# A gated recurrent kernel on one core: the biases and h0 on ScalarE's DMA queue, the banks zeroed from a tile of zeros

## The chip, the cores and the metric

The kernel runs on one core of a Trainium2 chip. The metric is the device time of one execution in microseconds (us), the median of several runs. A core has a matrix engine (TensorE, in the profile PE, with its weight loads as PEld), VectorE (DVE), ScalarE (ACT), GpSimd (POOL) and SyncE (SP). SP computes nothing here: it issues DMA transfers. [...]

## What is computed

The input x holds 8 sequences of 512 steps with 512 features; h0 is the first state, 8 by 512. Cut to what matters:

```
def step(h, x_t):
    fused = sigmoid(concat([x_t, h]) @ w_W + w_b)
    r, z  = split(fused, 2)
    m     = x_t @ wx_W + wx_b + r * (h @ wh_W + wh_b)
    h_new = z * h + (1 - z) * tanh(m)
    return h_new
out = x + all h_new, step after step
```

All of it is float32. The steps depend on each other. Only the products with x can be made ahead.

## The kernel before

The kernel's loop has 512 steps, one for each step of the sequences, all of the same work. The weights are kept in SBUF for the whole run: `wx` (for x) and `wh` (for h), each loaded by four DMAs of 768 KB, one for each quarter k of the 512 features. The units of the state lie in four quarters too: half A (`hTA`) and half B (`hTB`) hold two each. x comes in chunks of 16 steps (`xin`, 256 KB each, `load_x`, line 76), loaded three chunks ahead; the results go out in tiles `ot` of the same size.

A group is four steps. For each group, `seed` (line 155) copies the biases into a PSUM bank `xp`, `prefill` (line 159) adds x times `wx` to it, and `spread` (line 171) copies the parts to the banks A, B and Z, on which the products with h are summed. The banks alternate between groups. `turn_x` (line 176) transposes the part for the candidate state.

A step begins with 48 matmuls of h with `wh`, in the order of line 23, "A0 B0 A1 A2 A3 B1 B2 B3 Z0 Z1 Z2 Z3": the letter is the bank, the figure the quarter k of `wh` and of h. One quarter of the prefill for the group after next follows (`take(pre, 1)`, line 217). Then VectorE transposes the sums, ScalarE makes the sigmoids and the tanh, VectorE forms the new state by two scans (`memory`, line 261, `update`, line 281), half A before half B, and GpSimd adds x for the output. The next step's A0 waits for the new `hTA`, its A2 for the new `hTB`.

The loop's order is fixed by hand (line 199). The part ahead of it, the prologue, is ordered by a scheduler, in the order of the code where nothing else decides. There SP issues, by lines 83 to 96, 123 and 189: four transfers of biases (each a row of 512 values to 32 partitions), the first chunk of x, four of `wx`, four of `wh`, h0 (tile `hin`), and the next chunks of x. The DMAs have eight semaphores which they take in turn, so an issue can also wait for the transfer that had its semaphore before.

On the other engines the prologue does this. GpSimd sets `zeros`, the state tiles and some helper tiles to zero, VectorE the first `DVE_FILL` = 5 of the helper tiles (lines 111 to 115). VectorE copies `hin` into the first state (line 125). TensorE clears each of the eight PSUM banks with four matmuls, of a tile of zeros with the biases (line 143); this also marks the banks as begun, since all later matmuls only add. Then follow the seeds, the prefills of the first two groups and the spread of the first. ScalarE loads a table of functions ahead of its first copy (line 157) and another ahead of its first sigmoid (line 150).

Of the kernel before, what the change touches and what calls it, by code (L numbers as in the profile page):

```python
# [7 lines left out]
F32 = mybir.dt.float32  # L8
# [4 lines left out]
P = 128  # L13
NQ = 4
GS = 4
B = 8
HU = 64


DVE_FILL = 5  # L20
SYNC = mybir.DependencyInfo(mybir.DependencyClass.Sync, mybir.DependencyReason.DATA)

ORDER = "A0 B0 A1 A2 A3 B1 B2 B3 Z0 Z1 Z2 Z3"
# [7 lines left out]
def tile_cond_rnn_residual(  # L31
# [31 lines left out]
    nc = tc.nc  # L63
# [4 lines left out]
    const = ctx.enter_context(tc.tile_pool(name="const", bufs=1))  # L68
# [7 lines left out]
    def load_x(c):  # L76
        if c < NCH:
            t_ = xin_p.tile([P, NQ, TC * B], F32, tag="xin", name=f"xin_{c}")
            nc.sync.dma_start(out=t_, in_=x[c].rearrange("p (k n) -> p k n", k=NQ))  # L79
            xins[c] = t_  # L80


    bias = const.tile([P, 512], F32, name="bias")
    for j in range(NQ):
        nc.sync.dma_start(  # L85
            out=bias[32 * j : 32 * j + 32], in_=bias_d[j].partition_broadcast(32)
        )
    load_x(0)

    wx = const.tile([P, NQ, NQ, 384], F32, name="wx")  # L90
# [3 lines left out]
    wh = const.tile([P, NQ, NQ, 384], F32, name="wh")  # L94
    for k in range(NQ):
        nc.sync.dma_start(out=wh[:, k], in_=wh_d[:, k])

    NH = 2 * GS  # L100
    hT = [
        [const.tile([P, 32, 2, 2], F32, name=f"hT{n}{i}") for i in range(NH)]
        for n in "AB"
    ]
# [3 lines left out]
    hd0 = [[const.tile([P, B, 2, 2], F32, name=f"hd0{n}{i}") for i in range(2)] for n in "AB"]  # L108
    hd1 = [[const.tile([P, B, 2, 2], F32, name=f"hd1{n}{i}") for i in range(2)] for n in "AB"]
    zs = [[const.tile([P, 2, B], F32, name=f"z{n}{i}") for i in range(2)] for n in "AB"]  # L110
    zeros = const.tile([P, 32], F32, name="zeros")
    for t_ in [zeros] + hT[0] + hT[1]:
        nc.gpsimd.memset(t_, 0.0)
    for n, t_ in enumerate(hd0[0] + hd0[1] + md0[0] + md0[1]):
        (nc.vector if n < DVE_FILL else nc.gpsimd).memset(t_, 0.0)

# [2 lines left out]
        s = i % GS  # L119
        return hT[hf][i % NH][:, B * s : B * s + B, :, 1]  # L120

    hin = const.tile([P, NQ, B], F32, name="hin")
    nc.sync.dma_start(out=hin, in_=h0)
    for hf in range(2):
        nc.vector.tensor_copy(  # L125
            state(hf, 0), hin[:, 2 * hf : 2 * hf + 2].rearrange("p c b -> p b c")
# [8 lines left out]
    def mm(out_, lhsT, rhs, start=False):  # L135
        nc.tensor.matmul(  # L136
            out_, lhsT, rhs, start=start, stop=False, skip_group_check=True
        )


    for t_ in xps + list(banks[0].values()) + list(banks[1].values()):
        for j in range(NQ):
            mm(t_[32 * j : 32 * j + 32, :], zeros, bias[:, : t_.shape[1]], start=True)

# [39 lines left out]
                return  # L186
            n = None if n is None else n - 1

    load_x(1)
    load_x(2)  # L190
    for g in range(2):
        seed(g)
        take(prefill(g))
# [191 lines left out]
```

## Time and profile before

| | us |
|---|---|
| median of 3 runs | 1726.7 |
| lowest and highest run | 1726.22, 1728.58 |
| profiled execution | 1726.31 |
| its span, first to last instruction | 1724.5 |
| TensorE busy | 1706.2 |
| VectorE, ScalarE, GpSimd busy | 1138.6, 894.8, 252.9 |
| first matmul of the loop | 22.80 |

Times in the profile are counted from the start of the span. In a timeline, a row has start, length, engine, line, operation, output and inputs, count, and in brackets how long the engine was idle before it and what ended that. "SPq" is SP's queue issuing DMAs. The chain of waits follows the execution back from its last instruction, at each step to what released it. The granted clock (PEclk) is 1.00 at full speed of TensorE. All matmuls of the kernel have line 136, that of a helper, so they are told apart by tile: A, B, Z for the banks, xp for the prefill.

### The profile page before, as it was taken

Reading aid. Unit: us, or ns where it says so; the run is one execution under the profiler, and the core shown is the slowest. Engines: PE = TensorE matmul, PEld = TensorE weight load, DVE = VectorE, ACT = ScalarE, POOL = GpSimd, SP = SyncE. Lnnn points to the kernel's source line nnn. Section 1 sums busy time; section 2 is a strip of 40 time slices with the busy share of each in tenths; the row PEclk is TensorE's granted clock in tenths of the full one; section 3 lists DMA queues with packets and bytes.
Section 4 is the critical chain, followed back from the end, with each engine's and each line's share of the span. In section 5 each row is a group of like instructions: output and inputs, shape, how many; then the busy total and the mean of one; then the engine's idle time right before and its main releaser. Section 6 shows DMA issues by size and latency. Waiting matters only on the chain.

```text
span 1724.5 us, 121032 instructions
## 1 busy us (share of the span) xinstructions
PE 1706.2 (99%) x53312; PEld 1489.8 (86%) x53312; DVE 1138.6 (66%) x6663; ACT 894.8 (52%) x4610; POOL 252.9 (15%) x1048
## 2 busy tenths in 40 slices
PE   7999999999999999999999999999999999999998
PEld 5888888888888888888888888888888888888887
DVE  2666666666666666666666666666666666666666
ACT  3555555555555555555555555555555555555554
POOL 1111111111111111111111111111111111111111
PEclk9999999999999999999999999999999999999999
DMA  4000000000000000000000000000000000000000
GB/s 179 17 4 17 17 17 17 10 11 17 17 17 16 5 17 17 17 16 5 17 17 17 17 17 5 17 17 17 17 4 17 16 17 16 5 17 11 11 11 10
DMA packets 11232, 31.09 MB, mean 18 GB/s; under 512 B 1360, under 2 KB 1360, under 8 KB 10704
## 3 DMA queue, kind: packets, MB, share of 16 engines
q1 hardware_dynamic: 10704, 23.35, 3.9%
q8 instruction: 416, 6.82, 1.6%
q14 instruction: 112, 0.92, 0.2%
HBM read 14.96 MB, written 8.39 MB: 14 GB/s over the span
## 4 chain that ended last, share of the span: by engine, by line
PE 98%; DMA 1%; DVE 0%; issue 0%; SPq 0%; ACT 0%; POOLq 0%; POOL 0%; DVEq 0%
PE A L136 39%; PE B L136 25%; PE xp L136 19%; PE Z L136 14%; DMA hin<-in_h_dram 1%; DMA wx<-in_wx_dram 0%; DVE tr L231 0%; ACT md0A L150 0%; DVE hTA L283 0%; DVE m L263 0%; SPq L85 0%; DVE md L243 0%; SPq L79 0%; POOLq L379 0%; POOL ot L314 0%
## 5 line engine op out<-in xcount | busy, mean ns | idle before, releaser
L136 PE MATMUL A<-wh,hTA 128*32 128x192 f32 x8192 | 555.6, 327 | 9.5 <-DVE hTB L125 7.3
L136 PEld LDWEIGHTS A<-wh,hTA 128*32 128x32 f32 x8192 | 321.3, 137 | 184.6 <-DVE hTA L283 176.2
L136 PE MATMUL B<-wh,hTA 128*32 128x128 f32 x8192 | 450.9, 273 | 0.0
L136 PE MATMUL A<-wh,hTB 128*32 128x192 f32 x8192 | 448.3, 327 | 0.0
L136 PE MATMUL xp<-wx,xin 128*32 128x384 f32 x4096 | 444.2, 486 | 0.0
L231 DVE STREAM_TRANSPOSE tr<-A 128x64 f32<-128x64 f32 x512 | 128.0, 250 | 470.0 <-PE A L136 470.0
L150 ACT ACTIVATE md0A<-tr 128x16 f32<-128x16 f32 x512 | 121.1, 236 | 487.9 <-DVE tr L231 487.9
L136 PEld LDWEIGHTS B<-wh,hTA 128*32 128x32 f32 x8192 | 364.7, 136 | 1.6
L136 PE MATMUL B<-wh,hTB 128*32 128x128 f32 x8192 | 336.4, 273 | 0.0
L136 PEld LDWEIGHTS A<-wh,hTB 128*32 128x32 f32 x8192 | 302.4, 137 | 33.0 <-DVE hTB L283 1.2
L314 POOL TENSOR_TENSOR ot<-xin,hTA 128x16 f32<-128x16 f32 x512 | 125.5, 245 | 1119.5 <-DVE hTA L283 1031.6
L136 PEld LDWEIGHTS B<-wh,hTB 128*32 128x32 f32 x8192 | 266.6, 137 | 0.0
L136 PE MATMUL Z<-wh,hTB 128*32 128x64 f32 x8192 | 240.6, 226 | 0.0
L136 PE MATMUL Z<-wh,hTA 128*32 128x64 f32 x8192 | 235.0, 223 | 0.0
L136 PEld LDWEIGHTS Z<-wh,hTA 128*32 128x32 f32 x8192 | 218.5, 141 | 0.0
L136 PEld LDWEIGHTS Z<-wh,hTB 128*32 128x32 f32 x8192 | 200.1, 148 | 0.0
L314 POOL TENSOR_TENSOR ot<-xin,hTB 128x16 f32<-128x16 f32 x512 | 124.5, 243 | 348.5 <-DVE hTB L283 343.2
L150 ACT ACTIVATE md0B<-tr 128x16 f32<-128x16 f32 x512 | 119.2, 233 | 70.8 <-DVE tr L231 0.7
L283 DVE TENSOR_TENSOR_SCAN hTB<-hd0B,hd1B 128x32 f32<-128x32 f32 x512 | 115.2, 225 | 52.7
L263 DVE TENSOR_TENSOR_SCAN m<-md0B,md 128x32 f32<-128x32 f32 x512 | 147.6, 288 | 0.0
L243 DVE STREAM_TRANSPOSE md<-B 128x64 f32<-128x64 f32 x512 | 146.9, 287 | 0.0
L243 DVE STREAM_TRANSPOSE md<-A 128x64 f32<-128x64 f32 x512 | 139.0, 271 | 0.0
(43 smaller groups left out, 1835.8 us busy)
## 6 DMA issues: line engine op xcount, KB each, us to landing
xin<-in_x_dram SPq DMA_DIRECT2D x32, 256.0 KB, 2.9
out_dram<-ot SPq DMA_DIRECT2D x32, 256.0 KB, 2.1
wx<-in_wx_dram SPq DMA_DIRECT2D x4, 768.0 KB, 6.7
wh<-in_wh_dram SPq DMA_DIRECT2D x4, 768.0 KB, 13.5
bias<-in_bias_dram SPq DMA_DIRECT2D x4, 64.0 KB, 2.0
hin<-in_h_dram SPq DMA_DIRECT2D x1, 16.0 KB, 14.8
```

The costliest lines, as they stand in the source:

```text
L136: nc.tensor.matmul(out_, lhsT, rhs, start=start, stop=False, skip_group_check=True)
L150: inst = nc.scalar.activation(*args, **kw).ins
L231: nc.vector.transpose(t_.rearrange("p c n -> p (c n)"), raw[n][hf])
L243: inst = nc.vector.transpose(md1[g % 2][:, hf, :, :, 0].rearrange("p n c -> p c n"), raw["h"][hf]).ins
L263: nc.vector.tensor_tensor_scan(flat(m), flat(md0[hf][g % 2][:, rows]), flat(md1[g % 2][:, hf, rows]), 0.0, ALU.mult, ALU.add,)
L283: nc.vector.tensor_tensor_scan(flat(hT[hf][(i + 1) % NH][:, B * s1 : B * s1 + B]), flat(hd0[hf][i % 2]), flat(hd1[hf][i % 2]), 0.0, ALU.mu ...
L314: pool_done[i + 1] = nc.gpsimd.tensor_tensor(ot[:, 2 * hf : 2 * hf + 2, t, :].rearrange("p c n -> p n c"), xins[c][:, 2 * hf : 2 * hf + 2, ...
```

## The change

The four transfers of biases, and the one of h0, are issued by ScalarE's queue instead of SP's, and h0 directly after the biases. The second and third chunk of x are asked for in the code directly after `wh`. The tile `zeros` is 512 wide instead of 32, is filled by VectorE, and stands on both sides of the matmuls that clear the banks, so the biases are no longer read there. `DVE_FILL` goes from 5 to 4: with it the first tile `md0A`, the input of the first candidate scan, is cleared by GpSimd.

```diff
-DVE_FILL = 5
+DVE_FILL = 4
...
     bias = const.tile([P, 512], F32, name="bias")
     for j in range(NQ):
-        nc.sync.dma_start(
+        nc.scalar.dma_start(
             out=bias[32 * j : 32 * j + 32], in_=bias_d[j].partition_broadcast(32)
         )
+    hin = const.tile([P, NQ, B], F32, name="hin")
+    nc.scalar.dma_start(out=hin, in_=h0)
     load_x(0)
...
     for k in range(NQ):
         nc.sync.dma_start(out=wh[:, k], in_=wh_d[:, k])
+    load_x(1)
+    load_x(2)
...
-    zeros = const.tile([P, 32], F32, name="zeros")
-    for t_ in [zeros] + hT[0] + hT[1]:
+    zeros = const.tile([P, 512], F32, name="zeros")
+    nc.vector.memset(zeros, 0.0)
+    for t_ in hT[0] + hT[1]:
         nc.gpsimd.memset(t_, 0.0)
...
-    hin = const.tile([P, NQ, B], F32, name="hin")
-    nc.sync.dma_start(out=hin, in_=h0)
...
-            mm(t_[32 * j : 32 * j + 32, :], zeros, bias[:, : t_.shape[1]], start=True)
+            mm(t_[32 * j : 32 * j + 32, :], zeros[:, :32], zeros[:, : t_.shape[1]], start=True)
...
-    load_x(1)
-    load_x(2)
     for g in range(2):
         seed(g)
         take(prefill(g))
```

## The prediction

> **What bounds the kernel now.** I read the page first (its busy shares, then its chain of waits), then the timeline of the first 28 us, then the chain and the windows of that stretch.
>
> ```profile
> PE 1706.2 (99%) x53312; PEld 1489.8 (86%) x53312; DVE 1138.6 (66%) x6663; ACT 894.8 (52%) x4610; POOL 252.9 (15%) x1048
> PE 98%; DMA 1%; DVE 0%; issue 0%; SPq 0%; ACT 0%; POOLq 0%; POOL 0%; DVEq 0%
> ```
>
> TensorE makes up 98% of the chain, and that is the loop: 512 steps of about 3.31 us each (the distance of the transposes of A in the timeline). The diff touches nothing inside the loop, so only the prologue can move the end. Its DMA issues and the moments that matter, from the timeline:
>
> ```profile
> 0.74 1.78 SPq L85 DMA_DIRECT2D bias<-in_bias_dram  x4
> 2.56 0.42 SPq L79 DMA_DIRECT2D xin<-in_x_dram  x1
> 4.93 2.06 SPq L96 DMA_DIRECT2D wh<-in_wh_dram  x4
> 7.62 0.33 SPq L123 DMA_DIRECT2D hin<-in_h_dram  x1
> 9.51 4.09 SPq L79 DMA_DIRECT2D xin<-in_x_dram  x3
> 16.80 1.28 ACT L150 ACT_TABLE_LOAD   x1
> 26.07 0.25 DVE L231 STREAM_TRANSPOSE tr<-A 128x64 f32<-128x64 f32 x1 [3.31 <-PE A L136]
> 26.36 0.24 ACT L150 ACTIVATE md0A<-tr 128x16 f32<-128x16 f32 x1 [8.27 <-DVE tr L231]
> 27.30 0.23 DVE L283 TENSOR_TENSOR_SCAN hTA<-hd0A,hd1A 128x32 f32<-128x32 f32 x1
> ```
>
> See three things here. SP spends 1.78 us on issuing biases before the first x. The later chunks of x (9.51) are already issued behind wh (4.93). And the activation table for the sigmoid is loaded at 16.80, long before the first sigmoid needs it at 26.36. The chain of the same stretch:
>
> ```profile
> 7.62 14.81 DMA hin<-in_h_dram
> 22.80 0.88 PE A L136 x8
> 23.67 0.43 PE B L136 x8
> 24.10 1.92 PE A L136 x24
> 26.02 0.77 PE B L136 x24
> 26.79 0.49 PE Z L136 x32
> 27.28 0.64 PE xp L136 x8
> 27.92 0.33 PE A L136 x8
> ```
>
> The 16 KB of h0 land 14.81 us after their issue, at 22.43, since they stand behind all of wh. Step 0 then runs from 22.80 to 27.92. What wh itself does, from the view of that tensor, for its last two issues (6.0 and 6.5 us):
>
> ```profile
> DMA to landing us min/median/max: 14.2/15.0/15.7
> ```
>
> So wh3 lands at 6.5 + 15.7 = 22.2, only 0.2 us ahead of h0. This is the main reading: h0 is named by the chain, but the weights bind. The windows (columns: stretch, length, busy us of PE, PEld, DVE, ACT, POOL, then granted clock, DMA share, GB/s):
>
> ```profile
> 15.89:19.30 3.41, 0.00 (x0) 0.00 (x0) 0.22 (x3) 1.87 (x2) 0.00 (x0) 1.00 1.01 416
> 19.30:22.72 3.42, 0.00 (x0) 0.00 (x0) 0.20 (x2) 0.00 (x0) 0.00 (x0) 0.50 0.87 330
> 22.72:26.13 3.41, 3.33 (x48) 2.61 (x52) 0.10 (x2) 0.00 (x0) 0.00 (x0) 0.50 0.02 7
> 26.13:29.54 3.41, 3.41 (x113) 2.90 (x109) 2.29 (x13) 1.79 (x9) 0.49 (x2) 1.00 0.02 5
> ```
>
> The DMA engines are full until the weights are in. TensorE's clock fell to half during its idle time, and stayed there for the first 3.33 us of step 0.
>
> [...]
>
> **The change part by part.**
>
> 1. Biases leave SP's queue. SP's first issue becomes xin0, at 0.74 instead of 2.56, so the stream of x, wx and wh starts 1.8 us earlier. The four bias transfers don't vanish: 256 KB at the stream's 416 GB/s is 0.6 us. In the kernel before they moved before the stream; now they share the engines with it. That gives back 0 us (if they fill the stream's first latency) to 0.6 us. I take 0.6. wh3 then lands at 22.2 - 1.8 + 0.6 = 21.0. wh0 lands at 15.1 (4.9 + 10.2, the shortest of the four); three transfers more at 768 KB/416 GB/s = 1.9 us would take 5.7 us, and they took 7.1. The other 1.4 us I put down to one instruction fetch of 16 KB that the DMA view shows in 14.5 to 18. [...] I keep it.
>
> 2. h0 leaves SP's queue and the end of the stream. It is issued on ScalarE after the biases at about 2.6, and VectorE's two copies (0.18 and 0.17 us at 22.5) become free. This takes away the named wait, but the next is 1.2 us earlier at best (22.2 to 21.0), because wh3 is late next.
>
> 3. What starts without wh3. The matmuls of step 0 stand in the order A0 B0 A1 A2 A3 ..., one chunk of wh each. With h0 there, A0, B0, A1 and A2 run as wh0, wh1, wh2 land (the stream moved by 1.2: about 14, 17 and 19 us). Before, they cost 0.88 + 0.43 + 1.28 = 2.6 us after 22.80; now only A3 stands after wh3. A3 at half clock is 1.92/3 = 0.64 (24 rows are three quarters k of A), plus 0.24 of start (0.88 less 0.64): A ends at 21.05 + 0.88 = 21.9, against 26.02. Behind it B1 to B3, Z and xp took 0.77 + 0.49 + 0.64 = 1.90 at full clock. At half clock they take 3 x 0.43 + 2 x 0.43 + 2 x 0.64 = 3.4. Step 1 starts at 21.9 + 3.5 = 25.4 instead of 27.92: a gain of 2.5, if the half clock lasts just that long (4.4 us from 21.05).
>
> 4. The clock. A1 and A2 are 0.3 to 0.6 us of work in stretches of 2 us, so I expect half clock when wh3 lands: in 1719.14 to 1722.55 the same view has 0.78 us of TensorE, and the clock still fell after it (mean 0.76 in 1721 to 1724). [...] the half clock lasts 3.4 us from 21.05 at best and 6.8 at worst, mean 5.1. Each us of it costs half a us of work: the gain is 2.5 + 0.5 = 3.0, 2.5 - 1.2 = 1.3, and 2.15 in the mean.
>
> 5. Later chunks of x behind wh. Nothing: the issue order is already so, and in the changed program's order SP has x0, wx, wh, x1, x2. xin1 is first needed by the prefill in step 8, some 27 us into the loop.
>
> 6. Banks zeroed from zeros. TensorE's first matmul waits for one memset of 128x512 on VectorE. The 128x128 one takes 0.17 and the 128x32 one 0.09 to 0.12, so about 0.4 us, up at 1.3, in place of the biases at 4.30. The zeroing (32 matmuls, 4.30 to 9.6) starts 3 us earlier and the prefill follows the landing of wx. It ends near 13.2 (before: 15.49). All of this is hidden under the wait for wh, which is the cover: alone it saves nothing; were wh early, it would save up to 3 us. Memsets of GpSimd: one of 32 columns goes, one of 128 (0.20) comes, over by 3.7 us, hidden by the same.
>
> 7. The table load moves. The fill of the first md0A goes from VectorE to GpSimd (DVE_FILL 4), so the first sigmoid waits for two engines. In the changed program's order ScalarE waits for VectorE's transpose of A first, then loads the table, then waits for GpSimd. Before, the load had no wait ahead of it. So 1.28 us stand between the transpose and the sigmoid in step 0; behind them queue zA, hd0A, tanh, and VectorE's scan. hTA comes 26.02 to 27.53 = 1.51 us after A; now 1.51 + 1.28 = 2.8, at 24.7. At half clock TensorE is busy with B, Z and xp until 25.4, so the load is hidden; at full clock it costs up to 1.3[...]. In the best clock case (window done at 24.45) xp ends at 24.9 and some 0.15 is lost. I take 0, range 0 to 0.9.
>
> ScalarE's five DMA issues (2.1 us by SP's rate of 0.45 each) end at 2.9, before its first wait ends at 4.2. Hidden.
>
> Sum: -2.2 us, against the profiled execution's own 1726.31 (span 1724.5 and 1.8 around it): 1724.1. The median of the runs is 1726.7, 0.4 above it; [...] I sum from it with the mean clock of the changed kernel.
>
> **The rivals.** (A) as above. (B) The stream ends earlier: the biases hide in its first latency, or the late engine isn't late; 0.6, 1.4 or 2.0 us more, of which I take 1.3: 1722.8. (C) The clock stays full through the short bursts: A ends at 21.5, xp at 23.3, but then the table load shows: hTA at 21.5 + 2.8 = 24.3, step 1 at about 24.6, a gain of 3.3: 1723.0. Against it speaks the window with 0.78 us. (D) The gain stays away: bias and x packets slow each other, or the clock rises late (6.8 us)[...]: gain 0.5 to 1, 1725.6. (E) Slower: SP's issue of wx2 now waits on a semaphore that ScalarE's first bias transfer returns, in the changed program. SP's queue holds x0, wx0 and wx1 until then, about 4.4 us of stream, to some 7 us. If ScalarE's transfers start late, the stream starves, one us lost for each us; past a bias landing of 9.2 (7 plus the gain of 2.2) the kernel is slower. At 10.5 it would be 1727.6. Before, the first bias landed 2 us after its issue, which speaks against it.
>
> **How the numbers follow.** A 0.58, B 0.13, C 0.12, D 0.13, E 0.04. A alone spans 1723.1 to 1725.3: gains of 3.0 to 1.3, with 0.2 to 0.3 for wh3's landing. The range runs from 1722.5, taking in most of B and C, to 1725.9, over D. Two tenths of a per cent, about what a measurement of this kernel can tell from no change, is 3.5 us, so faster means under 1723.2: a tenth of A, most of B and two thirds of C, 0.27 with a little for a gain that I don't see. Slower by that much needs more than E: 0.04. The rest, 0.69, is within.
>
> **What would show it.** h0 lands before 7 us and no longer ends the chain; wh3's landing near 21.0 does; A0, B0, A1 and A2 run apart before it. The transpose of A starts near 22 instead of 26.07. A table load of 1.28 us stands between that transpose and the first sigmoid. Step 1 starts between 24.5 and 26.5. Steps stay at 3.31 us. I am wrong if wh3 lands outside 20.4 to 21.6, if the clock at 21 us is full, or if the steps change.

## The result, and the profile after

The changed kernel takes 1723.17 us in the median (1722.18 to 1724.39, 13 runs), the kernel before 1727.14 us in the same measurement (1726.22 to 1728.97, 13 runs). The ratio is 0.9976, with a 95% interval of 0.9967 to 0.9984: 0.24% or 4.0 us faster. In a second measurement (`r_after` below) it is 1722.35 against 1725.76, ratio 0.9981 (0.9973 to 0.9989). The forecast was 1724.1, within 1722.5 to 1725.9.

The profiled executions are 1726.31 before and 1723.64 after, 2.67 us apart. First the chain of waits of the changed kernel, in the prologue (start, length, what):

```profile
2.12 6.55 DMA bias<-in_bias_dram
...
8.68 12.54 DMA wh<-in_wh_dram
...
21.26 0.70 PE A L139 x8
21.97 1.28 PE B L139 x24
23.25 0.85 PE Z L139 x32
24.10 1.14 PE xp L139 x8
25.24 0.33 PE A L139 x8
```

h0 is gone from it. The biases stand in it because SP's last issue, that of wh3 (the last quarter of wh), waits for the semaphore of the last bias transfer; the DMA engines were full meanwhile (share 1.02 in 3.50 to 8.70 us, 1.00 in 8 to 10 us), so this cost nothing. The last quarter of wh ends the wait now, at 21.22, and only one group of A (8 rows, k = 3) stands behind it, where the chain before had all four from 22.80. Step 1 starts at 25.24 instead of 27.92: 2.68 us earlier, the whole difference of the two executions. From there on nothing changed: the mean step from the ninth on is 3.3118 us before and 3.3116 after. Now the timeline of the same stretch:

```profile
1.45 3.40 PE L139 MATMUL xp<-zeros 128*32 128x512 f32 x16 [1.45 <-DVE zeros L116]
8.76 1.28 ACT L160 ACT_TABLE_LOAD   x1 [8.76 <-DMA bias<-in_bias_dram]
10.69 7.06 PE L139 MATMUL xp<-wx,xin 128*32 128x384 f32 x64 [4.53 <-ACT xp L160]
22.02 0.25 DVE L232 STREAM_TRANSPOSE tr<-A 128x64 f32<-128x64 f32 x1 [3.63 <-PE A L139]
22.35 1.28 ACT L153 ACT_TABLE_LOAD   x1 [3.28 <-DVE tr L232]
24.45 0.23 DVE L284 TENSOR_TENSOR_SCAN hTA<-hd0A,hd1A 128x32 f32<-128x32 f32 x1
```

The transpose of A is at 22.02 (before 26.07), the table load stands behind it, and hTA is ready at 24.68, while TensorE is busy until 25.24. One thing was not expected: the biases land at 8.67 and the prefill begins at 10.69, a microsecond later than before (9.67), although the banks are cleared 3 us earlier. In between TensorE had nothing to do for 4.53 us; its clock was at half (0.50) from 11.31 to 14.72, and the 64 matmuls of the prefill took 7.06 us where they had taken 5.82. From the DMA views, KB each and median us to landing, of the kernel before:

```profile
bias<-in_bias_dram SPq DMA_DIRECT2D x4, 64.0 KB, 2.0
```

and of the changed kernel:

```profile
bias<-in_bias_dram ACTq DMA_DIRECT2D x4, 64.0 KB, 5.1
hin<-in_h_dram ACTq DMA_DIRECT2D x1, 16.0 KB, 8.0
```

### The profile page after: what moved, and what is told of

It is laid out like the page before. It is cut to its first block, busy times and chain, and to the rows that moved or that the text cites. A ratio compares the mean times of both kernels' runs of the same rounds, so it can differ in the third digit from the quotient of the medians.

```text
span 1721.9 us, 121031 instructions
## 1 busy us (share of the span) xinstructions
PE 1707.1 (99%) x53312; PEld 1484.6 (86%) x53312; DVE 1138.9 (66%) x6663; ACT 894.6 (52%) x4610; POOL 254.6 (15%) x1048
## 4 chain that ended last, share of the span: by engine, by line
PE 98%; DMA 1%; DVE 0%; issue 0%; ACT 0%; ACTq 0%; POOLq 0%; POOL 0%
PE A L139 39%; PE B L139 25%; PE xp L139 19%; PE Z L139 14%; DMA wh<-in_wh_dram 1%; DMA bias<-in_bias_dram 0%; DVE tr L232 0%; ACT md0A L153 0%; DVE hTA L284 0%; DVE m L264 0%; DVE md L244 0%; ACTq L85 0%; POOLq L380 0%; POOL ot L315 0%; DVE hd1A L275 0%
## 5 line engine op out<-in xcount | busy, mean ns | idle before, releaser
L153 ACT ACTIVATE zB<-tz 128x16 f32<-128x16 f32 x512 | 110.8, 216 | 53.9
```

The source lines that it names most:

```text
L153: inst = nc.scalar.activation(*args, **kw).ins
```

## The experiments

All twelve were timed beside the kernel before; a ratio is to it, in the same measurement. Its median there lay at 1725.8 to 1726.0, 1.2 to 1.4 us under that of the first measurement, so ratios are compared and not times across measurements. "Changed" means the changed kernel.

**`e1_bias_back`: the biases on SP again.**

```diff
-        nc.scalar.dma_start(
+        nc.sync.dma_start(
             out=bias[32 * j : 32 * j + 32], in_=bias_d[j].partition_broadcast(32)
```

> The changed kernel with the four bias transfers back on SP's queue, ahead of x; h0 stays on ScalarE's. My theory: the landing of the last quarter of wh ends the prologue, so this costs what the stream starts later: wh3 at 22.2 instead of 21.2, the transpose of A in step 0 near 23.0 instead of 22.0, 1724.2 us. Rival: the gain is that of h0 alone, which the chain of waits named: then nothing is lost, 1723.2 us.

Measured: 1723.34 us, ratio 0.9985 (0.9979 to 0.9992), 2.6 us under the kernel before and 0.7 to 1.6 us over the changed one by its two ratios (0.9981 and 0.9976). Its chain:

```profile
6.47 15.43 DMA wh<-in_wh_dram
...
21.94 0.88 PE A L139 x8
```

wh3 lands 0.7 later than in the changed kernel (21.22), less than the 1.0 expected, and still ends the prologue. So moving h0, with the biases left on SP, brings most of the gain, since it frees three of the four groups of A; moving the biases brings the rest. The intervals of the ratios overlap, so the second part is shown by the landing rather than by the times.

**`e2_h0_back`: h0 behind wh again.**

```diff
+    hin = const.tile([P, NQ, B], F32, name="hin")
+    nc.sync.dma_start(out=hin, in_=h0)
     for hf in range(2):
...
-    nc.scalar.dma_start(out=hin, in_=h0)
```

(The two later chunks of x stand behind it, as in the kernel before.)

> The changed kernel with h0 back on SP's queue behind wh (and the later chunks of x behind h0); the biases stay on ScalarE's. My theory: h0 lands at about 21.4, the first matmul of the loop starts at 21.7, and A0 to A2 stand on the path again: step 0 about 1.1 us ahead of the kernel before, 1726.0 us. Rival (the gain is the earlier start of the stream alone): 1723.2 us.

Measured: 1726.1 us, ratio 1.000 (0.9992 to 1.0008). The gain is gone; the 1 us that I expected to stay doesn't show, though it would still lie within the interval of 1.4 us to either side. The timeline of the profiled execution and, below the dots, its chain:

```profile
25.26 0.25 DVE L232 STREAM_TRANSPOSE tr<-A 128x64 f32<-128x64 f32 x1 [3.30 <-PE A L137]
25.59 1.28 ACT L151 ACT_TABLE_LOAD   x1 [6.73 <-DVE tr L232]
27.69 0.22 DVE L284 TENSOR_TENSOR_SCAN hTA<-hd0A,hd1A 128x32 f32<-128x32 f32 x1
...
27.34 0.80 PE xp L137 x8
28.14 0.39 PE A L137 x8
```

Step 0 does start 0.8 us earlier than before (at 21.99, before at 22.80), and the transpose of A is 0.8 us earlier. After that, two things delay step 1. The table load, which the change put there, takes 1.28, so that hTA is ready at 27.91, after the 27.53 of the kernel before. And the half clock lasted until 27.52 (before: 26.13), so that TensorE itself was at work until 28.14, where step 1 starts; by the chain it was this that set the start here, 0.2 us later than the load would have. Which of the two takes the gain in the other runs is not shown. So h0's move is necessary, and the earlier stream brings nothing measurable without it.

**`e3_fill5`: md0A cleared by VectorE again.**

```diff
-DVE_FILL = 4
+DVE_FILL = 5
```

> The changed kernel with DVE_FILL 5 again, so that the first md0A is cleared by VectorE and the table load has no wait ahead of it. My theory: in the changed kernel the load lies beside TensorE's half-clock work, so that 0 to 0.4 us is won: 1723.0 us. Rival: its 1.28 us are on the path: 1721.9 us.

Measured: 1722.34 us, ratio 0.9979 (0.9970 to 0.9988), equal to the changed kernel within the intervals; the runs spread over 3 us (1720.36 to 1723.52). This doesn't decide alone. Its profile, one of the fastest of its runs (1721.22), shows the clock at full through the whole of step 0; from its windows (columns as in the prediction):

```profile
17.82:21.23 3.41, 1.69 (x40) 1.02 (x40) 0.54 (x4) 2.07 (x4) 0.00 (x0) 1.00 0.98 391
21.23:24.65 3.42, 3.42 (x108) 2.86 (x112) 2.23 (x13) 1.80 (x9) 0.48 (x2) 1.00 0.07 23
```

and from those of the changed kernel:

```profile
18.13:21.55 3.42, 1.41 (x35) 0.74 (x28) 0.26 (x3) 0.59 (x1) 0.00 (x0) 1.00 0.92 364
21.55:24.96 3.41, 3.41 (x72) 2.59 (x68) 1.53 (x10) 2.29 (x7) 0.15 (x1) 0.50 0.04 13
```

The same work, cut by stretches that fall otherwise: behind the one with 1.69 us of TensorE the clock was 1.00, behind the one with 1.41 it was 0.50 for 3.41 us.

**`e4_zero_back`: the banks cleared with the biases again.**

```diff
-            mm(..., zeros[:, :32], zeros[:, : t_.shape[1]], start=True)
+            mm(..., zeros[:, :32], bias[:, : t_.shape[1]], start=True)
```

> The changed kernel, but the banks are cleared with the biases as the moving operand again, so TensorE waits for the biases, which land at 8.7. My theory: the clearing starts at 8.7 and the prefill ends near 18.5, A0 to A2 fit before wh3 lands at 21.2, and since TensorE has less idle time its clock may be full then: 1722.5 to 1723.2 us. Rival: the earlier clearing is where the gain is from: 4 us later prefill, 1725 us or more.

Measured: 1722.36 us, ratio 0.9981 (0.9973 to 0.9989), equal to the changed kernel. The prefill runs from 13.06 to 18.41 instead of 10.69 to 17.75, and A0 to A2 still end before wh3 lands at 21.18. The earlier clearing of the banks brings nothing measurable. The clock was full from 11.39 on, and then the table load was in the chain (22.18 to 23.47), with step 1 at 24.56.

**`r_after`: the changed kernel again.**

> The changed kernel itself once more, beside the others of this call. Theory of the clock's windows: its profile falls in another place of the windows, so the half clock after wh3's landing lasts between 0 and 5 us; the times spread over some 2 us, and the ratio to the kernel before stays between 0.997 and 0.9985. If the half clock is tied to the kernel and not to free windows, its profile is as the first: half from about 21.5 to 25.0 us.

Measured: ratio 0.9981 (0.9973 to 0.9989). In its profile the clock fell at 22.04, 0.86 us after wh3's landing (0.3 in the first profile), after a stretch of 3.41 us with 1.38 us of TensorE. A3 ran at full clock, the half clock lasted into step 1 (25.46), and step 1 started at 24.82, 0.4 us earlier than in the first profile. So the place of the half clock is not fixed by the kernel: 21.55 to 24.96 in the first profile, 22.04 to 25.46 in this one.

**`e6_hold` and `e7_hold_fill5`: the clock kept up, without and with the table load out of the way.** Both put matmuls of zeros into the waits of step 0, which add zeros to bank xp1; the second also has DVE_FILL 5.

```diff
+HOLD = {"A2": (384,), "A3": (512, 192)}
...
+            for w in HOLD.get(n, ()) if i == 0 else ():
+                for j in range(NQ):
+                    mm(xps[1][32 * j : 32 * j + 32, :w], zeros[:, :32], zeros[:, :w])
```

> The changed kernel with three groups of matmuls of zeros put into TensorE's waits ahead of A2 and A3 of step 0 (they add zeros to a bank). Theory: [...] its clock is full when wh3 lands in every run; A ends at 21.6, but the table load is then on the path and step 1 starts at 24.6 instead of 25.05: 0.4 to 0.8 us faster than the changed kernel in the median, with a smaller spread. Rival: the clock does not matter, because the table load lies beside it anyway: no difference.

> The same matmuls of zeros, and DVE_FILL 5, so neither the half clock nor the table load is in step 0. Theory: step 1 starts at 23.3 in every run, 1.2 us ahead of the hold alone and 1.7 us ahead of the changed kernel. Rival: the load costs nothing, and this is equal to the hold alone.

Measured: 1721.31 us, ratio 0.9973 (0.9963 to 0.9983), and 1720.23 us, ratio 0.9967 (0.9955 to 0.9979). The clock was full in both profiles: 1.00 in 18.62 to 22.03 of the first, with 3.16 us of TensorE, and 24 rows of B took 0.66 in the second, where the changed kernel at half clock has 1.28. The chains differ as expected. With the hold alone, ScalarE's load is in it:

```profile
22.13 1.28 ACT L154
...
24.51 0.56 PE A L140 x8
```

With DVE_FILL 5, TensorE runs through:

```profile
22.95 0.65 PE xp L140 x8
23.60 0.33 PE A L140 x8
```

Between the two lies 1.1 us in the medians and 0.9 in these chains: at full clock the table load costs that, while in the changed kernel, at half clock, hTA was ready at 24.68, ahead of the end of TensorE's work at 25.24. The spread fell from 2.4 us (`r_after`, 14 runs) to 0.6 and 0.4 (8 and 6 runs). The step of the expectation that failed: of the 1.0 us between the hold and `r_after`, 1.4 are in the loop (mean step 3.3080 against 3.3108 us, times 504), not in step 0. Within what these runs tell, full clock with the table load on the path (step 1 at 24.51) was worth as much here as half clock with the load hidden (24.82 in `r_after`).

**`e5_wide_clear`: fewer instructions ahead of the loop.**

```diff
-        for j in range(NQ):
-            mm(t_[32 * j : 32 * j + 32, :], zeros[:, :32], zeros[:, : t_.shape[1]], start=True)
+        mm(t_, zeros[:, :P], zeros[:, : t_.shape[1]], start=True)
```

> The changed kernel, but each bank is cleared by one matmul with 128 columns of zeros as weights instead of four with 32, so 96 of the 128 instructions of the clearing are gone. Theory that the fetch of TensorE's instructions delays one DMA engine by 1.4 us: the fetch now comes only after TensorE is past its wait for wh3, wh3 lands at 19.8 instead of 21.2, and the kernel is about 1.4 us faster, 1.4 to 1.9 if less idle time also keeps the clock up. Rival (the late engine has another cause, such as its place in the memory): wh3 stays at 21.2 and the time the same.

Measured: 1719.84 us (1719.65 to 1720.00), ratio 0.9965 (0.9952 to 0.9977), 2.5 us under `r_after` in the same measurement. The chain:

```profile
8.17 11.73 DMA wh<-in_wh_dram
...
19.94 0.60 PE A L139 x8
```

wh3 lands 1.3 us earlier, and the fetch that the trace had at 14.5 to 14.7 in the changed kernel now comes at 21.1. This supports the fetch as what makes one DMA engine late; the last section has the other profiles on it. The rest of the 2.5 is again in the loop: mean step 3.3080.

**`e10_before_wide`: the same edit in the kernel before.** There it is `mm(t_, zeros, bias[:, : t_.shape[1]], start=True)` with zeros of 128 columns.

> The kernel before with one change: each bank is cleared by one matmul with 128 columns of zeros. Theory of the instruction fetch: it moves behind TensorE's wait for h0, so the weights and h0 land 1.4 us earlier, at 20.8 and 21.0, and step 0 starts at 21.4: 1.4 us faster than the kernel before. Rival (the late engine belongs to the order of the changed kernel or to the place of wh in memory): no difference.

Measured: 1723.23 us, ratio 0.9983 (0.9977 to 0.9990), 2.7 us faster, twice the expected gain. wh3 landed at 20.84 and h0 at 21.02, step 0 started at 21.39: 1.4 us earlier, as expected. In this profile, the slowest of its 21 runs, the half clock lasted until 27.26, so step 1 started only 0.2 us earlier than before; the mean step of 3.3078 instead of 3.3118 gives 2.0 us over the loop. This one edit in the prologue's TensorE work, with nothing of the change, is worth 0.7 to 0.9 of what the change is, by the ratios (0.9983 against 0.9976 and 0.9981).

**`e11_wide_padded`: what is in the loop?** This is `e5_wide_clear`, but the 24 matmuls that it saves come back as matmuls of zeros where TensorE is idle under the table load.

```diff
         take(pre, 1)
+        for _ in range(6) if i == 0 else ():
+            for j in range(NQ):
+                mm(xps[1][32 * j : 32 * j + 32, :HU], zeros[:, :32], zeros[:, :HU])
```

> The wide clearing, with the 24 matmuls that it saves given back as matmuls of zeros behind the prefill of step 0, where TensorE is idle for 1 us under the table load; so the number of TensorE's instructions from step 1 on is that of the changed kernel. Theory: the wide clearing has two gains; the landing of wh3 at 19.9 stays, but the four to seven long steps (3.4 to 4.0 us, each the second step of a chunk of 16) come back[...]: mean step 3.310 to 3.312 us and 1721.2 us, 1.4 above the wide clearing alone. Rival: the long steps belong to the matmuls of the old clearing or to chance: mean step 3.308 us and 1719.8 us.

Measured: 1721.61 us, ratio 0.9976 (0.9967 to 0.9985). wh3 landed at 19.99, so the prologue's gain stayed; the mean step is 3.3098, and long steps are back. Counted are steps over 3.4 us after the eighth, from the distances of the transposes of A:

| kernel | long steps | mean step, us |
|---|---|---|
| before; changed; `r_after` | 6; 6; 5 | 3.3118; 3.3116; 3.3108 |
| `e1`; `e2`; `e3`; `e4` | 4; 3; 4; 4 | 3.3103; 3.3108; 3.3100; 3.3108 |
| `e5`; `e6`; `e7`; `e8`; `e9`; `e10` | 0; 0; 1; 0; 0; 0 | 3.3080; 3.3080; 3.3083; 3.3076; 3.3079; 3.3078 |
| `e11` | 3 | 3.3098 |

Each of them is the second step of a chunk of 16. They go, but for one in `e7`, wherever TensorE's instructions ahead of the loop are other in number, and come back when the number does. Each count is from one execution.

**`e8_wide_fill5` and `e9_wx_pieces`.** The first is the wide clearing with DVE_FILL 5, the second the same with the rows of wx padded.

```diff
-    wx = const.tile([P, NQ, NQ, 384], F32, name="wx")
+    wx = const.tile([P, NQ, NQ, 400], F32, name="wx")
...
-        nc.sync.dma_start(out=wx[:, k], in_=wx_d[:, k])
+        nc.sync.dma_start(out=wx[:, k, :, :384], in_=wx_d[:, k])
```

(The matmuls of the prefill read `wx[:, k, j, :384]` to match.)

> The changed kernel with the wide clearing of the banks and DVE_FILL 5. Theory: the wide clearing brings wh3 to 19.9 with a full clock, where the table load is wholly on the path; with DVE_FILL 5 the load is early and step 1 starts at 22.0 instead of 23.3: 1.2 us under the wide clearing alone, 7 us under the kernel before. Rival: something else is late at once (the scan for half B, say) and at most 0.4 us is won.

> As the wide clearing with DVE_FILL 5, but the rows of wx in SBUF are padded from 384 to 400 values, so that wx comes in pieces of 1536 bytes instead of 6144, in the same four DMAs. Theory: [...] with pieces of a quarter of the size the biases land at about 5 us instead of 8.2 and the prefill starts at 7 to 8; the time is the same within 0.4 us, since wh3 still ends the prologue. Rival (ScalarE's queue is slow by itself[...]): the biases land at 8 again.

Measured: `e8_wide_fill5` 1719.18 us, ratio 0.9962 (0.9950 to 0.9975). It is the fastest of all by its ratio, 6.7 us under the kernel before, but not told apart from the wide clearing alone (0.9965): by the medians 0.7 us of the expected 1.2. In its profile wh3 came at 20.31, 0.4 later than in `e5`, and step 1 started at 22.70 instead of 23.27, so the table load is off the path, as expected. `e9_wx_pieces` 1719.97 us, ratio 0.9964 (0.9952 to 0.9976), with runs from 1717.45 to 1722.48. Its DMA view:

```profile
bias<-in_bias_dram ACTq DMA_DIRECT2D x4, 64.0 KB, 4.8
hin<-in_h_dram ACTq DMA_DIRECT2D x1, 16.0 KB, 6.2
```

The pieces of wx were 1536 bytes, and the last bias landed at 8.3 all the same. So smaller pieces of wx did not bring the biases to the 5 us that I had expected; h0, behind them, came 1.6 us sooner than in the changed kernel (9.0 against 10.6). Why a transfer on ScalarE's queue takes 3 to 8 us beside SP's stream stays open: the issues themselves took 0.44 us each in the changed kernel, where SP's of the kernel before took 0.41, and h0 alone on ScalarE's queue, at 0.73 in `e1`, landed in 2.1 us, beside the small bias transfers alone. In this profile, the slowest of its runs, the fetch came at 19.1, while TensorE waited for wh3, and wh3 landed at 21.96: the late engine was back.

## Why the prediction was right, point by point

The forecast of the path holds: the prologue moved, the loop didn't, and wh3 replaces h0 as what ends it. The account of the clock does not: full clock at 21 us was named as a sign of being wrong, and it came, in the changed kernel (full until 21.55) and in `r_after` (until 22.04).

1. **Biases leave SP's queue.** wh3 was forecast for 21.0 and landed at 21.2; `e1` shows what it is without the move, 21.9. The price of the bias bytes on the shared engines was rightly taken as real: of the 1.8 us by which the stream starts earlier, wh3 keeps 1.0, so the price is 0.8 where I took 0.6. In the first 20 us ScalarE's queue (q10: the biases and h0) has 4.4% of the 16 engines' time, 0.9 us. The fetch, which I kept with 1.4 us, is still there with some 1.1: wh1 lands 3.05 us after wh0, the next two 1.8 and 1.9 apart.
2. **h0.** The named wait is gone, and the gain it leaves is that of A0 to A2. The forecast of its landing (before 7 us) was wrong: 10.6.
3. **What starts without wh3.** The transpose of A was forecast near 22 and came at 22.02. Step 1 was forecast for 25.4 and started at 25.24.
4. **The clock is the mis-sized term.** I held that it is at half when wh3 lands, and for 5.1 us in the mean. That mean, and its bounds of 3.4 and 6.8 us, were my estimate; the trace of the kernel before has a single half clock ahead of the loop's second step, of 6.83 us, 3.33 of them in step 0. In the changed kernel's two profiles it was full then, fell 0.3 and 0.9 us later and stayed so for 3.4 us; in `e3`, with the same matmuls, it didn't fall behind that landing. The mean of those three is 2.3 us of half clock instead of 5.1, by my estimate 1.4 us of time. The half clock of the kernel before was taken from its one profile, 3.3 us; its median is 0.8 above that profile's time in the same measurement. Together these two are 2.2 us and would turn the forecast gain of 2.2 into 4.4; the medians give 4.0 and, in the second measurement, 3.4. That 1724.1 came within 0.5 us of the profiled execution is in part luck: with 2.3 us of half clock the same sum gives 1722.7. Rival C, a clock kept up by the short bursts, is what some of the runs are: `e4`, which it fits, starts step 1 at 24.56, where C had 24.6.
5. **Later chunks of x** were behind wh already. No run tests it alone, and none needs to: SP's issue order is wx, wh, x in both timelines.
6. **Clearing from zeros** was forecast to be hidden, and `e4` shows it. The stated cover, the wait for wh, is real but thinner than I thought, since the prefill waits for the biases. It ended at 17.75, not at 13.2, in part at half clock. "ScalarE's five DMA issues ... Hidden" failed as put: the issues are hidden, the landings held ScalarE until 8.76, not 4.2. It cost nothing because TensorE still waited 2.0 us for wh within step 0.
7. **The table load** was forecast as hidden at half clock, up to 1.3 us at full clock. `e7` against `e6` has 1.1 at full clock; in `e2`, at half clock, it was hidden by 0.2 us. No more than the load is seen: the sigmoid starts 0.01 us after it ends (23.63 and 23.64).

Rival E, a starved stream, is refuted: the first bias landed at 3.57, and SP's wx2, which waits for it, was issued at 3.59, when two transfers of wx were still queued. The later issues waited in the same way, wh3's until 8.68, and the DMA engines stayed full (share 1.02 in 3.50 to 8.70 us).

## What to carry to other kernels

Where a wait is named for a small transfer at the end of a queue, look at what lands just ahead of it (here wh3, 0.2 us ahead of h0); moving the small one is worth what can start in between (here A0 to A2; step 1 starts 2.68 us earlier), and the large one is the next bound. A first function of a new table behind a wait can drag its table load onto the path (1.28 us here, of which `e6` against `e7` lost 1.1), and a change of who fills a buffer was enough to do that. In a kernel of thousands of small matmuls, the prologue's instruction count can be a tuning parameter of its own (24 matmuls fewer in `e5`, 2.5 us less): count the long steps before crediting an edit with a gain.

## What the runs showed of the hardware that was not expected

**The granted clock.** In these traces the half clock (0.50) of the prologue and of the loop's first steps lasts 3.41 us or a multiple of that: 19.30 to 26.13 in the kernel before, 11.31 to 14.72 and 21.55 to 24.96 in the changed one, 17.70 to 27.93 in `e1`. The stretches of the table are 3.41 us long, laid out from such a change:

| kernel and stretch | TensorE busy, us | clock after it |
|---|---|---|
| before, 1719.14 to 1722.55 | 0.78 | falls to half |
| `e1`, 14.29 to 17.70 | 1.20 | falls to half |
| before, 2.23 to 5.65 | 1.35 | stays full |
| `r_after`, 18.63 to 22.04 | 1.38 | falls to half |
| changed, 18.13 to 21.55 | 1.41 | falls to half |
| `e5`, 5.29 to 8.70 | 1.58 | falls to half |
| `e3`, 17.82 to 21.23 | 1.69 | stays full |
| `e4`, 18.21 to 21.63 | 2.03 | stays full |
| `e1`, 21.11 to 24.52 | 2.58 | stays half |
| before, 22.72 to 26.13 | 3.33 | rises to full |

So from half it rose behind 3.33 us and stayed behind 2.58, by the modelled busy times of these profiles. For the fall they give no single limit: it came behind 1.58 us in `e5` and stayed away behind 1.35 in the kernel before. What counts beside the busy time is not shown.

**Instruction fetches stand beside two losses.** The first is in the loads. In ten of the fourteen profiles a fetch of 16 KB starts between 13.1 and 19.1 us, while wh is under way; the quarter of wh that lands next comes 2.6 to 3.3 us after the transfer ahead of it, and every other quarter 1.8 to 2.0 us. In the changed kernel the fetch is at 14.70, and its packet takes 1.03 us. The late quarter is wh1, for which 15 of the 16 DMA engines are done by 16.31 and the last at 17.52; in wh2 and wh3 the last one is behind the others again, by 1.21 and 1.26 us (18.13 and 19.34, 19.96 and 21.22). In the kernel before the fetch is at 15.24 and the late one wh1, in `e4` it is at 16.52 and the late one wh2; in `e9`, 19.09 and wh3. In the four profiles without such a fetch (`e5`, `e8`, `e10`, `e11`) none is late; wh3 landed 1.3 us earlier in `e5` than in the changed kernel, and 1.4 earlier in `e10` than in the kernel before. And in the loop, in the long steps, TensorE stands in the middle of a row of matmuls with nothing to wait for, as in this line of the kernel before, in a step of 4.02 us:

```profile
1408.61 0.11 PEld L136 LDWEIGHTS xp<-wx,xin 128*32 128x32 f32 x2 [0.63 <-issue]
```

A fetch had begun 2.3 us earlier, at 1406.28, while the chunk's load of 256 KB was under way (it landed at 1408.29). That TensorE lacks what this fetch brings is not shown; shown is only that the long steps go and come with the number of instructions ahead (`e5` and `e10` against `e11`), and that they are worth 0.9 to 2 us over the loop.
